# Four graph layers on one core: scores copied in halves of two batches, `gd` and `z` loads held to the product 40 back, the turned adjacency loaded beside layer one, partial rows added by VectorE

## The chip, the cores and the metric

The kernel runs on one core of one Trainium2 chip. The metric is the device time in microseconds; three runs give 3038.36, 3040.70 and 3043.71, a median of 3040.7 us. TensorE (PE) multiplies, VectorE (DVE) and ScalarE (ACT) work element by element, GpSimd (POOL) issues indirect DMAs (gathers and scatters by a list of rows) and SyncE (SP) issues most plain DMAs. All data are float32, and a product of the kernel appears in the trace as two matmuls.

## The reference, cut to what matters

`x` has 16 batches of 1024 nodes with 256 features; `adj` is 1024 x 1024 and sparse, with a diagonal. Four layers follow one another.

```python
# layer 0: a score for every edge
pre_u = h_t @ W1[:d]; pre_v = h_t @ W1[d:]
hidden = relu(pre_u[:, :, None, :] + pre_v[:, None, :, :] + b1)
S = sigmoid((hidden @ W2)[..., 0] + b2[0])
a_t = einsum('buv,bud->bvd', S * A_a, h_t)
m_t = einsum('uv,bud->bvd', A_m, h_t) * h_t
z = beta1 * h_t + beta2 * (a_t @ Wa + ba) + beta3 * (m_t @ Wm + bm)
# layer 1: neighbours
z = z + relu(einsum('ij,bjd->bid', adj, z) @ W.T + b)
# layers 2 and 3: attention with adj as the bias of the logits
feats = data @ W1.T; f1 = feats @ W2 + b2[0]
coefs = softmax(leaky_relu(f1[:, :, None] + f1[:, None, :]) + adj)
out = coefs @ feats + bias2 + data
```

## The kernel before, in words

The batches are taken in four groups of four (`GB = 4`). Layer 0's scores are worked out for edges alone: each node has 16 listed neighbours of its own (`FIRST`) and, where it has more, extra rows of four (`QUAD`). The score steps (`score_steps`) gather a neighbour's features (`z<-v_d`), take maxima and minima on VectorE (L1066 to L1068), add them up on ScalarE (L1034) and scatter the scores into one of two dense arrays in DRAM (`dense_d`, L951). They run as a side thread: `Side.along` lets the main work yield its estimated time and issues as many side steps as a pace allows. So the order of issue comes from the order of these generators, from explicit waits that hold an instruction to a product some places back (`paced(ins, back)`, 6 unless said otherwise), and from when buffers come free. Each engine, and each engine's own DMA queue, works in order.

A first stage (to about 906 us) does all that needs no score: it turns `adj` (`turn_adj`, into `adjT_d`, with its block sums in `sumT_d`), makes `m_t` and projects the features for all 16 batches (`hw_d`, `zb_d`). Its tiles (`own1`, `st`) are then given up, and their room goes to later pools. Then each group does, in order:

- **The scores** (`with_edges`, for group 3 `with_last_edges`). Four quarters `v` of 256 columns, in each eight steps `ut` of 128 rows. A step loads a block `gd` of scores from `dense_d` (`load_gd`, on SP, four buffers, held to the product 24 back), where the four batches lie interleaved; copies it into `gc`, batch by batch (ScalarE at L1499 for steps 0, 1, 3 and 5, VectorE at L1497 for 2, 4, 6 and 7, two buffers); and makes eight products with `hw`, two for each batch. After a quarter VectorE adds the eight sums to `z` (L1522). In some steps a load of `z` is issued behind the products, held to the product 12 back. Group 0 also loads the turned `adj` over `adj_sb` here (L1514, held to the product 16 back) and takes its exponential on ScalarE (L1484), for the attention layers.
- **Layer one**, for two batches at a time: `projected` makes y (8 steps), then seven block products (`neighbours_by_seven`, 28 steps) take the blocks of the turned `adj` from a stream of loads on SP (`adj_stream`): whole blocks into `blocks`, parts of 512 KB into `gc`, single pieces of 256 KB into `a`.
- **Two attention layers** (`fronts`, `sums`, `second`, `third`, in `group_layers`). A front's row of logits goes to DRAM and back, spread over all partitions (`to_row`, L1405 to L1407 on SP), and is used by `from_row` (L1412) some steps later. `later` holds calls that `tick` makes after a number of steps. The loads of the next group's `hw`, `z` and first four `gd` are issued here; `soon` asks for those `gd` between the halves of the group's last sums, if the next group's scores are all issued (`finished`).

The last group differs: two of its batches get layer one from lists (`by_lists`), beside the main work of the other two. 24 + 112 steps gather rows of y (`z<-y_d`) and add them, weighted, on VectorE (L1805, L1807); then 28 GpSimd DMAs (L1817) gather partial rows from `part_d` and add them into `msg` themselves (`compute_op=ALU.add`). Every step yields 1.0 and the main work gives 0.71 for each of its microseconds (`LISTED`). `from_lists` then turns `msg` on TensorE (L1830).

Of the kernel before, what the change touches and what calls it, by code (L numbers as in the profile page):

```python
# [81 lines left out]
def gnn_stack_kernel(  # L82
# [48 lines left out]
    recent = []  # L131
    BACK = 24

    def paced(ins, back=6):
# [6 lines left out]
    def product(*args, **kw):  # L141
        recent.append(nc.tensor.matmul(*args, **kw))  # L142
        del recent[:-BACK]
        return recent[-1]
# [780 lines left out]
    with tc.If(listed > 0) as arm:  # L925
        with ExitStack() as stack:
# [11 lines left out]
            gd_pool = stack.enter_context(tc.tile_pool(name="gd", bufs=4, reuse_waits="tile"))  # L938
            gc_pool = stack.enter_context(tc.tile_pool(name="gc", bufs=2, reuse_waits="tile"))
            searched = set()  # L940
# [230 lines left out]
            with ExitStack() as first:  # L1171
                own1 = first.enter_context(tc.tile_pool(name="own1", bufs=1, reuse_waits="tile"))
                st_pool = first.enter_context(tc.tile_pool(name="st", bufs=5, reuse_waits="tile"))
                side = Side(score_steps(own1))
                pools = (wide_t, wide_z)
# [10 lines left out]
                def spare_tile(tag):  # L1186
                    pool = dict(gd=gd_pool, gc=gc_pool)[tag]
                    shape = [P, QN, GB] if tag == "gd" else [P, GB, QN]
                    return pool.tile(shape, F32, tag=tag, name="sums").rearrange("p a b -> p (a b)")

                def last_plain(h, hT, mT):

                    for q, tag in ((S3, "gc"), (S1, "gd"), (S2, "gd")):
# [38 lines left out]
                def score_free():  # L1232
# [45 lines left out]
                    def first_turned(main):  # L1278
                        for us in itertools.islice(main, 4):
                            if turned_adj:  # L1280
                                what = turned_adj.pop(0)
                                if what[0] < HT - 1:
                                    room = [spare_tile("gc" if what[0] == 2 else "gd") for _ in range(2)]
                                else:
                                    room = list(ttile("sums")[:, : 2 * N].rearrange("p (k n) -> k p n", k=2))
# [59 lines left out]
                assert not zeros  # L1345

            two = stack.enter_context(tc.tile_pool(name="two", bufs=2, reuse_waits="tile"))
            three = stack.enter_context(tc.tile_pool(name="three", bufs=3, reuse_waits="tile"))
# [133 lines left out]

            def exponential(jt):
                paced(nc.scalar.activation(ea[:, jt, :], ea[:, jt, :], AF.Exp), 16)  # L1484

            def with_edges(g, hw, z):

                doing[0] = "edges"
                for v in range(N // QN):
                    cols = slice(v * QN, (v + 1) * QN)  # L1490
                    acc = [[bank() for _ in range(DH)] for _ in range(GB)]
                    for ut in range(NT):
                        gd = first_gd.pop(0) if first_gd else load_gd(g, v, ut, back=BACK)
                        gc = gc_pool.tile([P, GB, QN], F32, tag="gc", name="gc")
                        by_batch = gd.rearrange("p n i -> p i n")
                        if ut in (2, 4, 6, 7):
                            paced(nc.vector.tensor_copy(gc, by_batch), 16)  # L1497
                        else:
                            paced(nc.scalar.activation(gc, by_batch, AF.Copy), 16)  # L1499
                        for i in range(GB):  # L1500
                            for eh in range(DH):
                                product(
                                    acc[i][eh][:, :QN], hw[i][:, ut, eh * P : (eh + 1) * P], gc[:, i, :],
                                    start=ut == 0, stop=ut == NT - 1,
                                )
                        if z_loads and ut % 2 == 0:
                            load, *what = z_loads.pop(0)
                            paced(load(*what), 12)
                        if (to_load or to_exp) and ut % 2 and v:
                            if v > 1 and to_exp:  # L1510
                                exponential(to_exp.pop(0))
                            if to_load:
                                jt = to_load.pop(0)
                                paced(nc.sync.dma_start(ea[:, jt, :], adjT_d[jt]), 16)  # L1514
                                to_exp.append(jt)
                        yield 3.4 if g or v else 1
                    if v == N // QN - 1:
                        while to_exp:
                            exponential(to_exp.pop(0))
                    for i in range(GB):  # L1520
# [15 lines left out]
            def with_last_edges(g, hw, z, rows):  # L1536
# [27 lines left out]
                for v in (0, 2, 1, 3):  # L1564
# [8 lines left out]
                    for ut in range(NT):  # L1573
                        gd = first_gd.pop(0) if first_gd else load_gd(g, v, ut, back=BACK)
                        gc = gc_pool.tile([P, GB, QN], F32, tag="gc", name="gc")
                        by_batch = gd.rearrange("p n i -> p i n")
                        if v in held:
                            nc.vector.tensor_copy(gc[:, 2:, :], by_batch[:, 2:, :])
                            nc.scalar.activation(held[v][ut], by_batch[:, :2, :], AF.Copy)
                        elif ut in (2, 4, 6, 7):  # L1580
                            paced(nc.vector.tensor_copy(gc, by_batch), 16)
                        else:
                            paced(nc.scalar.activation(gc, by_batch, AF.Copy), 16)
                        for i in batches:
                            products(acc, i, ut, gc[:, i, :])
                        if z_loads and ut % 2 == 0:
                            load, *what = z_loads.pop(0)
                            paced(load(*what), 12)
                        yield 0.9 * len(batches)
# [72 lines left out]
            def adj_stream(room):  # L1662
# [14 lines left out]
                def ask(name, k, n=1, first=False):  # L1677
# [3 lines left out]
                    elif k < 2:  # L1681
                        a = gc_pool.tile([P, GB, QN], F32, tag="gc", name="adjT_in")
                        a, n = a.rearrange("p a b -> p (a b)").rearrange("p (k n) -> p k n", n=HN), 2
                    else:
# [85 lines left out]
            def by_lists(msg):  # L1770
# [13 lines left out]
                todo = [(NT + i, k) for i in range(XT) for k in range(QUAD)]  # L1784
                todo += [(t, k) for t in range(FAR) for k in range(FIRST)]
                got, stores, free = {}, [], []

                def fetch_row(t, k):
                    if not free:
                        free.extend(halves([slot_pool.tile([P, GB * R], F32, tag="z", name="z")]))  # L1790
                    z = got[t, k] = free.pop(0)
                    gather(z, y_d, lists(t)[1][:, k : k + 1])

# [5 lines left out]
                for n, (t, k) in enumerate(todo):  # L1799
# [3 lines left out]
                    to = msg[t] if t < NT else part[t % len(part)]  # L1803
                    if k == 0:
                        paced(nc.vector.tensor_scalar(to, z, lists(t)[3][:, k : k + 1], None, ALU.mult))  # L1805
# [8 lines left out]
                    yield 1.0  # L1814
                for q in range(NG):
                    for t in range(FAR):
                        gather(msg[t], part_d, to_u[:, q * NT + t : q * NT + t + 1], compute_op=ALU.add)  # L1817
                        yield 1.0

            def from_lists(z, msg):  # L1820
# [102 lines left out]
            def group_layers(g, z):  # L1923
# [21 lines left out]
                order = [(layer, i) for layer in range(2) for i in range(GB)]  # L1945
                yield from layer_one(z[:2])
                yield from fronts(0, 0, row=False)
                yield from layer_one(z[2:])
                for n, (layer, i) in enumerate(order):
                    if n + 1 < len(order):  # L1950
                        yield from fronts(*order[n + 1])
# [11 lines left out]
                catch_up()  # L1963

            def soon(g):

                if g in finished:
                    first_gd.extend(load_gd(g, 0, ut) for ut in range(4))

# [171 lines left out]
```

## Time and profile before

| what | value |
|---|---|
| median of three runs | 3040.7 us (3038.36 to 3043.71) |
| the profiled execution's own time | 3069.58 us |
| its span, first to last instruction | 3067.9 us |
| mean granted TensorE clock | 0.996 |
| TensorE matmul busy, weight load busy | 2990.1 us, 2140.8 us |
| VectorE, ScalarE, GpSimd busy | 2076.5, 1819.3, 1745.2 us |
| moved by DMA | 736.76 MB, 240 GB/s over the span |
| scores of groups 0, 1, 2, 3 | 909 to 1032, 1455 to 1574, 1998 to 2118, 2537 to 2641 us |
| end of the lists | 2849 to 2911 us |

How to read what is quoted. A row of waits gives the engine, the tile it wanted, who was waited for, then the time in all, how often, and the longest. A row of the timeline gives start, duration, engine (q: its queue, issuing a DMA), line, operation, tiles written and read, shapes, how many were merged, and in brackets the idle time ahead and who ended it. A row of windows gives the stretch, its length, busy time and count of PE, weight loads (PEld), VectorE, ScalarE and GpSimd, then the granted clock, the DMA share and GB/s. A row of groups gives line, engine, operation, tiles, shapes and count, then busy time and the mean of one in ns, then the idle time just before and what ended it. Most products have the line of a helper, L142.

### The profile page before, as it was taken

What the parts mean: (1) busy time and instruction counts of PE and PEld (TensorE: products, weight loads), DVE (VectorE), ACT (ScalarE), POOL (GpSimd) and SP (SyncE); (2) the same over time, 40 slices, a digit from 0 to 9 for tenths busy, and PEclk for the clock granted to TensorE, in tenths of its full rate; (3) what the DMA queues carried; (4) which work ended last, traced back from release to release, by engine and by line L of the source; (5) the groups of instructions that cost most, each with busy time, mean ns of one, the idle gap of its engine ahead of it and who ended that gap; (6) DMA issues with size and microseconds to landing.
All of it is one profiled execution on the core that took longest, in us unless ns stands there. A gap on an engine that the chain in (4) does not pass through costs nothing. (4 is left out here: it accounts for less than half of the span.)

```text
span 3067.9 us, 41621 instructions
## 1 busy us (share of the span) xinstructions
PE 2990.1 (97%) x11750; PEld 2140.8 (70%) x11750; DVE 2076.5 (68%) x4089; ACT 1819.3 (59%) x6466; POOL 1745.2 (57%) x1501
## 2 busy tenths in 40 slices
PE   8999999999999999999999999999999999999899
PEld 5545455555557657888775788787578888858787
DVE  8877566666665678887667788766777752478444
ACT  3437565667666767887766687776667733222342
POOL 1126577677654667667666767667666610467600
PEclk9999999999999999999999999999999999999999
DMA  9999999989899986578998666898866545676700
GB/s 296 315 353 329 306 306 301 278 251 279 252 337 342 298 265 183 173 215 283 301 294 270 188 181 194 284 306 288 273 195 167 151 159 181 230 234 175 144 1 29
DMA packets 324697, 736.76 MB, mean 240 GB/s; under 512 B 50973, under 2 KB 145242, under 8 KB 319338
## 3 DMA queue, kind: packets, MB, share of 16 engines
q0 software_dynamic: 131456, 394.14, 43.5%
q1 hardware_dynamic: 151610, 268.05, 26.3%
q10 hardware_dynamic: 41392, 71.84, 6.3%
q8 instruction: 94, 1.54, 0.2%
q14 instruction: 145, 1.19, 0.1%
HBM read 597.34 MB, written 136.53 MB: 239 GB/s over the span
## 5 line engine op out<-in xcount | busy, mean ns | idle before, releaser
L1034 ACT ACTIVATE z<-z 128x257 f32<-128x257 f32 x2432 | 984.1, 410 | 523.2 <-DVE z L1068 266.6
L142 PE MATMUL bank<-feats,m 128*128 128x257 f32 x4096 | 913.1, 381 | 13.9 <-DVE m L1465 4.5
L142 PEld LDWEIGHTS bank<-feats,m 128*128 128x128 f32 x4096 | 769.1, 190 | 128.6 <-DVE m L1465 6.7
L946 POOL DMA_INDIRECT z<-v_d,slot_v x512 | 606.4, 1184 | 403.4 <-ACT z L1034 162.4
L951 POOL DMA_INDIRECT dense_d<-gt,slot_at x512 | 588.1, 1149 | 221.7 <-PE bank L142 105.4
L1066 DVE TENSOR_TENSOR z<-z,u 128x580 f32<-128x580 f32 x608 | 460.9, 758 | 320.3 <-PE bank L142 228.5
L1465 DVE SCALAR_TENSOR_TENSOR m<-rho,tau,adj_sb 128x512 f32<-128x512 f32 x512 | 374.8, 745 | 143.2 <-PE bank L142 133.7
L1034 ACT ACTIVATION_READ_ACCUMULATOR z<-z 128x1 f32 x2432 | 467.2, 192 | 0.0
L142 PE MATMUL bank<-gc,hw 128*128 128x256 f32 x1920 | 422.2, 381 | 25.5 <-ACT gc L1499 20.3
L142 PEld LDWEIGHTS bank<-gc,hw 128*128 128x128 f32 x1920 | 361.3, 190 | 85.5 <-ACT gc L1499 28.0
L1067 DVE TENSOR_TENSOR z<-z,u 128x448 f32<-128x448 f32 x608 | 375.9, 618 | 0.0
L142 PE MATMUL bank<-w1p,hT 128*128 128x385 f32 x1024 | 340.1, 486 | 0.9 <-ACT hT L154 0.9
L142 PEld LDWEIGHTS bank<-w1p,hT 128*128 128x128 f32 x1024 | 193.1, 189 | 147.7 <-issue 22.0
L142 PE MATMUL bank<-g_wT,z 128*128 128x257 f32 x1024 | 231.3, 380 | 4.9 <-DVE z L1739 3.2
L142 PE MATMUL bank<-adj_sb,h 128*128 128x512 f32 x504 | 223.3, 593 | 0.1
L142 PEld LDWEIGHTS bank<-g_wT,z 128*128 128x128 f32 x1024 | 192.1, 190 | 36.5 <-issue 4.7
L373 ACT ACTIVATE st<-bank 128x385 f32<-128x385 f32 x256 | 122.3, 484 | 107.1 <-PE bank L142 67.7
L946 POOL DMA_INDIRECT z<-v_d,x_node x96 | 123.0, 1281 | 104.5 <-PE bank L142 43.9
L142 PEld LDWEIGHTS bank<-adj_sb,h 128*128 128x128 f32 x504 | 95.7, 190 | 115.6 <-issue 106.8
L1068 DVE TENSOR_TENSOR z<-z,sign 128x128 f32<-128x128 f32 x608 | 171.8, 283 | 0.0
L946 POOL DMA_INDIRECT z<-y_d,slot_v x112 | 124.0, 1107 | 45.8 <-issue 20.1
L142 PE MATMUL bank<-adjT_in,t 128*128 128x512 f32 x336 | 147.6, 592 | 0.0
(258 smaller groups left out, 3315.6 us busy)
## 6 DMA issues: line engine op xcount, KB each, us to landing
gd<-dense_d SPq DMA_DIRECT2D x128, 512.0 KB
dense_d<-zero ACTq DMA_DIRECT2D x64, 512.0 KB
h<-in_x_dram SPq DMA_DIRECT2D x19, 1024.0 KB
u_d<-st SPq DMA_DIRECT2D x128, 128.5 KB
v_d<-st SPq DMA_DIRECT2D x128, 128.5 KB
u<-u_d POOLq DMA_DIRECT2D x32, 514.0 KB
hw_d<-st SPq DMA_DIRECT2D x128, 128.0 KB
zb_d<-zb ACTq DMA_DIRECT2D x16, 1024.0 KB
```

The costliest lines, as they stand in the source:

```text
L142: recent.append(nc.tensor.matmul(*args, **kw))
L373: nc.scalar.activation(st[:, cols], ps[:, :half], AF.Copy)
L946: return paced(nc.gpsimd.indirect_dma_start(out=dst, out_offset=None, in_=src[:], in_offset=bass.IndirectOffsetOnAxis(ap=at, axis=0), **how,))
L951: return paced(nc.gpsimd.indirect_dma_start(out=dst[:], out_offset=bass.IndirectOffsetOnAxis(ap=at, axis=0), in_=src, in_offset=None,))
L1034: nc.scalar.activation(zk[:, c, :], zk[:, c, :], AF.Copy, accum_out=s[:, k, c : c + 1])
L1066: paced(nc.vector.tensor_tensor(big, big, uk[:, :, :BIG], ALU.max))
L1067: paced(nc.vector.tensor_tensor(low, low, uk[:, :, BIG:], ALU.min))
L1068: nc.vector.tensor_tensor(mixed, mixed, sign[:, None, :].to_broadcast([P, GB, MIXED]), ALU.mult)
L1465: nc.vector.scalar_tensor_tensor(m, r[:, cols], ta[:, kt : kt + 1], ea[:, kt, cols], ALU.max, ALU.mult)
```

## The change

- **Copies.** `gc` is now four buffers of two batches each, made after the first stage instead of before it, so that it lies where that stage's tiles were; the first stage's use of it goes to a pool `sums` of its own. Each step copies its scores in two halves on the same engine, held to the products 16 and 12 back, and a batch's products read the half that holds it. The stream's 512 KB loads into `gc` become two of 256 KB.
- **Holds.** The list of recent products keeps 40 (`DEEP`) instead of 24; `gd` and the `z` loads of the scores stages are held to the product 40 back, instead of 24 and 12.
- **Turned adj.** The eight loads and exponentials leave the scores of group 0 and go beside the first layer one of group 0 (`with_adj`): a load every fourth step, its exponential six steps later.
- **First gd.** `soon` is called from the sixth of a group's eight sums on, twice each, and issues the four loads once, spread over later steps.
- **Partial rows.** They are gathered into the tiles of the list steps, five steps ahead, and added into `msg` by VectorE.

The diff, its core:

```diff
+    DEEP = 40
     def product(*args, **kw):
         recent.append(nc.tensor.matmul(*args, **kw))
-        del recent[:-BACK]
+        del recent[:-DEEP]
...
-            gc_pool = stack.enter_context(tc.tile_pool(name="gc", bufs=2, reuse_waits="tile"))
...
+                sum_pool = first.enter_context(tc.tile_pool(name="sums", bufs=2, reuse_waits="tile"))
...
+            gc_pool = stack.enter_context(tc.tile_pool(name="gc", bufs=4, reuse_waits="tile"))
...
-            def exponential(jt):
-                paced(nc.scalar.activation(ea[:, jt, :], ea[:, jt, :], AF.Exp), 16)
+            def with_adj(main):
+                for n, us in enumerate(main):
+                    if n % 4 == 1 and to_load:
+                        jt = to_load.pop(0)
+                        paced(nc.sync.dma_start(ea[:, jt, :], adjT_d[jt]), 16)
+                        to_exp.append(jt)
+                    if n % 4 == 3 and len(to_exp) > (1 if to_load else 0):
+                        jt = to_exp.pop(0)
+                        paced(nc.scalar.activation(ea[:, jt, :], ea[:, jt, :], AF.Exp), 16)
+                    yield us
+
+            def by_batch(gd, ut):
+                gc = {}
+                for i in range(0, GB, 2):
+                    t = gc_pool.tile([P, 2, QN], F32, tag="gc", name="gc")
+                    scores = gd[:, :, i : i + 2].rearrange("p n i -> p i n")
+                    if ut in (2, 4, 6, 7):
+                        paced(nc.vector.tensor_copy(t, scores), 16 - 2 * i)
+                    else:
+                        paced(nc.scalar.activation(t, scores, AF.Copy), 16 - 2 * i)
+                    gc[i], gc[i + 1] = t[:, 0, :], t[:, 1, :]
+                return gc
...
                     for ut in range(NT):
-                        gd = first_gd.pop(0) if first_gd else load_gd(g, v, ut, back=BACK)
-                        gc = gc_pool.tile([P, GB, QN], F32, tag="gc", name="gc")
-                        by_batch = gd.rearrange("p n i -> p i n")
-                        if ut in (2, 4, 6, 7):
-                            paced(nc.vector.tensor_copy(gc, by_batch), 16)
-                        else:
-                            paced(nc.scalar.activation(gc, by_batch, AF.Copy), 16)
+                        gd = first_gd.pop(0) if first_gd else load_gd(g, v, ut, back=DEEP)
+                        gc = by_batch(gd, ut)
...
                         if z_loads and ut % 2 == 0:
                             load, *what = z_loads.pop(0)
-                            paced(load(*what), 12)
-                        if (to_load or to_exp) and ut % 2 and v:
-                            if v > 1 and to_exp:
-                                exponential(to_exp.pop(0))
-                            if to_load:
-                                jt = to_load.pop(0)
-                                paced(nc.sync.dma_start(ea[:, jt, :], adjT_d[jt]), 16)
-                                to_exp.append(jt)
+                            paced(load(*what), DEEP)
...
                     elif k < 2:
-                        a = gc_pool.tile([P, GB, QN], F32, tag="gc", name="adjT_in")
-                        a, n = a.rearrange("p a b -> p (a b)").rearrange("p (k n) -> p k n", n=HN), 2
+                        for i in range(2):
+                            a = gc_pool.tile([P, 2, QN], F32, tag="gc", name="adjT_in")
+                            a = ready[name, i] = a.rearrange("p a b -> p (a b)")
+                            load = nc.sync.dma_start(a, source(name)[:, i, :])
+                            if first:
+                                paced(load, BACK)
+                        return
...
                 todo += [(t, k) for t in range(FAR) for k in range(FIRST)]
+                todo += [(t, FIRST + q) for q in range(NG) for t in range(FAR)]
...
-                    gather(z, y_d, lists(t)[1][:, k : k + 1])
+                    if t < NT and k >= FIRST:
+                        at = (k - FIRST) * NT + t
+                        gather(z, part_d, to_u[:, at : at + 1])
+                    else:
+                        gather(z, y_d, lists(t)[1][:, k : k + 1])
...
-                    if k == 0:
+                    if t < NT and k >= FIRST:
+                        paced(nc.vector.tensor_tensor(to, to, z, ALU.add))
+                    elif k == 0:
...
-                for q in range(NG):
-                    for t in range(FAR):
-                        gather(msg[t], part_d, to_u[:, q * NT + t : q * NT + t + 1], compute_op=ALU.add)
-                        yield 1.0
...
-                yield from layer_one(z[:2])
+                yield from with_adj(layer_one(z[:2])) if g == 0 else layer_one(z[:2])
...
                 for n, (layer, i) in enumerate(order):
+                    if n >= 2 * GB - 3:
+                        soon(g + 1)
...
                     yield from sums(made[layer, i], 0, *ends)
-                    if n == 2 * GB - 1:
+                    if n >= 2 * GB - 3:
                         soon(g + 1)
...
             def soon(g):
-                if g in finished:
-                    first_gd.extend(load_gd(g, 0, ut) for ut in range(4))
+                if g in finished and g not in asked:
+                    asked.add(g)
+                    for ut in range(4):
+                        later.append([1 + 2 * ut, lambda ut=ut: first_gd.append(load_gd(g, 0, ut))])
```

More of the change, by code (lines that the diff above doesn't have):

```diff
@@ L1186, in spare_tile @@
                 def spare_tile(tag):
-                    pool = dict(gd=gd_pool, gc=gc_pool)[tag]
-                    shape = [P, QN, GB] if tag == "gd" else [P, GB, QN]
-                    return pool.tile(shape, F32, tag=tag, name="sums").rearrange("p a b -> p (a b)")
+                    pool = dict(gd=gd_pool, sums=sum_pool)[tag]
+                    return pool.tile([P, QN, GB], F32, tag=tag, name="sums").rearrange("p a b -> p (a b)")
                 def last_plain(h, hT, mT):
-                    for q, tag in ((S3, "gc"), (S1, "gd"), (S2, "gd")):
+                    for q, tag in ((S3, "sums"), (S1, "gd"), (S2, "gd")):
                         adj_sums[q] = [spare_tile(tag).rearrange("p (k n) -> p k n", n=HN) for _ in range(2)]
@@ L1282, in first_turned @@
                                 if what[0] < HT - 1:
-                                    room = [spare_tile("gc" if what[0] == 2 else "gd") for _ in range(2)]
+                                    room = [spare_tile("sums" if what[0] == 2 else "gd") for _ in range(2)]
                                 else:
@@ L1502, in with_edges @@
                                 product(
-                                    acc[i][eh][:, :QN], hw[i][:, ut, eh * P : (eh + 1) * P], gc[:, i, :],
+                                    acc[i][eh][:, :QN], hw[i][:, ut, eh * P : (eh + 1) * P], gc[i],
                                     start=ut == 0, stop=ut == NT - 1,
@@ L1507, in with_edges @@
                             load, *what = z_loads.pop(0)
-                            paced(load(*what), 12)
-                        if (to_load or to_exp) and ut % 2 and v:
-                            if v > 1 and to_exp:
-                                exponential(to_exp.pop(0))
-                            if to_load:
-                                jt = to_load.pop(0)
-                                paced(nc.sync.dma_start(ea[:, jt, :], adjT_d[jt]), 16)
-                                to_exp.append(jt)
+                            paced(load(*what), DEEP)
                         yield 3.4 if g or v else 1
-                    if v == N // QN - 1:
-                        while to_exp:
-                            exponential(to_exp.pop(0))
                     for i in range(GB):
@@ L1573, in with_last_edges @@
                     for ut in range(NT):
-                        gd = first_gd.pop(0) if first_gd else load_gd(g, v, ut, back=BACK)
-                        gc = gc_pool.tile([P, GB, QN], F32, tag="gc", name="gc")
-                        by_batch = gd.rearrange("p n i -> p i n")
+                        gd = first_gd.pop(0) if first_gd else load_gd(g, v, ut, back=DEEP)
                         if v in held:
[L1578 to L1581, printed above, removed]
+                            t = gc_pool.tile([P, 2, QN], F32, tag="gc", name="gc")
+                            nc.vector.tensor_copy(t, gd[:, :, 2:].rearrange("p n i -> p i n"))
+                            nc.scalar.activation(held[v][ut], gd[:, :, :2].rearrange("p n i -> p i n"), AF.Copy)
+                            gc = {2: t[:, 0, :], 3: t[:, 1, :]}
                         else:
-                            paced(nc.scalar.activation(gc, by_batch, AF.Copy), 16)
+                            gc = by_batch(gd, ut)
                         for i in batches:
-                            products(acc, i, ut, gc[:, i, :])
+                            products(acc, i, ut, gc[i])
                         if z_loads and ut % 2 == 0:
                             load, *what = z_loads.pop(0)
-                            paced(load(*what), 12)
+                            paced(load(*what), DEEP)
                         yield 0.9 * len(batches)
@@ L1945, in group_layers @@
                 order = [(layer, i) for layer in range(2) for i in range(GB)]
-                yield from layer_one(z[:2])
+                yield from with_adj(layer_one(z[:2])) if g == 0 else layer_one(z[:2])
+                assert not to_load and not to_exp
                 yield from fronts(0, 0, row=False)
@@ L1963, in group_layers @@
                 catch_up()
+            asked = set()
             def soon(g):
-                if g in finished:
-                    first_gd.extend(load_gd(g, 0, ut) for ut in range(4))
+                if g in finished and g not in asked:
+                    asked.add(g)
+                    for ut in range(4):
+                        later.append([1 + 2 * ut, lambda ut=ut: first_gd.append(load_gd(g, 0, ut))])
             def left_by(main):
```

## The prediction

> **What bounds the kernel now.** I read the page's busy table first, then TensorE's waits, then its timeline in the four scores stages and the tail, then the stage windows, and last the rows that price each edit.
>
> ```profile
> span 3067.9 us, 41621 instructions
> PE 2990.1 (97%) x11750; PEld 2140.8 (70%) x11750; DVE 2076.5 (68%) x4089; ACT 1819.3 (59%) x6466; POOL 1745.2 (57%) x1501
> ```
>
> TensorE (PE) is the bound: 2990.1 of 3067.9. No product is added or removed, so only the 77.8 us of idle time can shrink. Who ends it:
>
> ```profile
> PE bank L142 <- ACT gc L1499: 20.3, 16, 2.3
> PE bank L1830 <- DMA msg<-part_d,to_u: 9.8, 5, 3.6
> PE bank L142 <- DMA hw<-hw_d: 3.1, 1, 3.1
> ```
>
> The first two of these waits, the longest of all, are what the change touches: the ScalarE copy of the scores into `gc`, and the rows that a GpSimd DMA adds into `msg`. The stages, with PE busy ahead of the other engines:
>
> ```profile
> 909.00:1032.00 123.00, 110.45 (x503) 94.25 (x502) 69.40 (x129) 83.29 (x242) 60.01 (x50) 1.00 0.96 333
> 1032.00:1096.00 64.00, 64.00 (x187) 35.29 (x186) 43.93 (x85) 36.33 (x152) 43.20 (x39) 1.00 0.86 276
> 2537.00:2641.00 104.00, 104.00 (x486) 91.60 (x485) 30.39 (x53) 35.38 (x32) 1.01 (x2) 1.00 0.57 182
> 2849.00:2893.00 44.00, 43.67 (x218) 38.17 (x216) 20.44 (x42) 11.22 (x26) 36.13 (x23) 1.00 0.87 151
> 2892.60:2910.70 18.10, 8.14 (x34) 6.64 (x34) 5.46 (x10) 4.85 (x8) 8.36 (x6) 0.63 0.69 132
> ```
>
> They are the scores of group 0, its first layer one, the scores of group 3 (no score steps beside it, DMA 0.57, no idle at all), and the end of the lists. Summing the gaps in PE's timeline, the scores lose 12.55 us in group 0 (3.06 of it for `hw`), 6.32 in group 1 and 6.49 in group 2. In the waits above many carry ScalarE's name and are DMA waits underneath:
>
> ```profile
> 943.37 0.53 SPq L1163 DMA_DIRECT2D z<-zb_d  x1
> 945.10 0.33 SPq L1514 DMA_DIRECT2D adj_sb<-adjT_d  x1
> 945.52 5.38 SPq L1148 DMA_DIRECT2D gd<-dense_d  x2
> 947.78 2.02 ACT L1499 ACTIVATE gc<-gd 128x1024 f32<-128x1024 f32 x1 [2.09 <-DMA gd<-dense_d]
> 949.85 7.17 PE L142 MATMUL bank<-gc,hw 128*128 128x256 f32 x32 [1.75 <-ACT gc L1499]
> ```
>
> The SP queue holds a `z` load for the product 12 back and an `adj` load for the one 16 back, and the next `gd` waits behind them. Pairing issues with copies, a `gd` normally goes out 9.7 us before its first product and its copy starts 6.5 to 8.7 us after issue; between 938 and 972 in group 0 that takes 8.2 to 11.6 us, and one load early in each of groups 1 and 2 took 10.3 and 10.8. By cause the stalls are about 8.2 us of late `gd` (6.5 in group 0) and 14.1 us where the copy stood in ScalarE's queue.
>
> **The change part by part.** *gd and z at 40 back.* A product is two matmuls, 422.2/960 = 0.44 us, a step of eight products 3.5 us. 24 back gives 10 us of lead, 40 would give 17. Four `gd` buffers cap it at when the copy four steps earlier has ended, some 15 us. The worst landing above was 11.6, so the 8.2 us of late `gd` go. `z` at 40 back no longer holds what is behind it. Bounds: 0 (bandwidth alone sets the landing) to 8.2; I take 8, since 11.6 is well under 15.
>
> *Half copies.* Prices:
>
> ```profile
> L1499 ACT ACTIVATE gc<-gd 128x1024 f32<-128x1024 f32 x48 | 99.3, 2069 | 22.1 <-DMA gd<-dense_d 12.7 <-PE bank L142 6.8 <-issue 2.5
> L1579 ACT ACTIVATE held<-gd 128x512 f32<-128x512 f32 x16 | 18.2, 1138 | 28.1 <-DMA gd<-dense_d 27.9
> L1484 ACT ACTIVATE adj_sb<-adj_sb 128x1024 f32<-128x1024 f32 x8 | 8.4, 1046 | 0.0
> L1660 DVE TENSOR_TENSOR z<-z,r 128x512 f32<-128x512 f32 x8 | 5.5, 693 | 12.8 <-ACT r L1659 12.8
> ```
>
> Two halves cost ScalarE 2 x 1138 = 2276 ns for 2069, 0.2 us more on each of 56 copies, hidden where it is 68% busy. A whole copy could start only when the step two before had ended, leaving 3.5 - 2.07 = 1.4 us to spare. A half starts 1.7 us earlier and its user comes one half later: 3.5 + 1.7 - 1.14 = 4.1 us. No stall exceeded 2.3 us beyond the 1.4, 3.7 in all. But a copy also queues behind score sums, which are held to recent products, and at the ends of a quarter VectorE's eight adds to `z` come first: I take 8.5 of the 14.1 (bounds 0 and 14.1). The new buffers lie where `wm` lay and wait for its last products, some 1.2 us: hidden under the 3.06 us wait for `hw`, else that much.
>
> *Turned adj in layer one.* 8 loads of 0.52 MB and 8 Exp of 1.05 us leave the scores of group 0 (inside the above) and go beside 64 us with no PE gap. Each load waits for the product 16 back, 7 us old while y is projected and 14 in the seven products, so SP passes it at once. The loads ask for 4.19 MB/64 us = 66 GB/s beside 276 at share 0.86, so a share of about 1.07: some 4 us of transfers arrive later. Behind each on SP are the blocks of the adjacency stream, asked about two blocks (14 us) ahead. Bounds -1 to 12.6 us (4.19 MB at 333 GB/s, all exposed); I take +1. Splitting five 0.5 MB `gc` loads per layer one adds five issues of 0.3 to 0.4 us on SP, hidden there.
>
> *Early gd.* Scatters of group 1 end at 1355, of group 2 at 1921, so its first four loads move from one half ahead of the scores to three or four halves ahead, spread, past SP's `hw`, `z` and row loads. Idle at the two group ends is 9.0 us now; bounds -9 to +9; I take 0, the queue having 60 us for them. In group 3 the scatters end at 2470; a `gd` asked before that stands at SP's head until then, with `hw` and the row of the last front behind it, but that row goes out at 2484 now and `hw` has until 2537.
>
> *Partial rows by VectorE.* 28 GpSimd DMAs take 1.54 + 0.30 us each, 52 us from 2849 to 2902.5, and PE waits:
>
> ```profile
> 2892.07 0.60 PE L1880 MATMUL bank<-ident,z 128*128 128x128 f32 x4
> 2896.26 0.30 PE L1830 MATMUL bank<-ident,msg 128*128 128x128 f32 x1 [3.59 <-DMA msg<-part_d,to_u]
> ...
> 2910.64 8.99 PE L142 MATMUL bank<-g_wT,z 128*128 128x257 f32 x40
> ```
>
> From 2892.7 to 2910.6, 18 us pass for 32 transposes that take 0.13 us each elsewhere, 4.2 us. A plain gather of such a row takes 1.02 + 0.30 us (`z<-y_d`), under the 1/0.71 = 1.41 us of a list step, and is asked five steps ahead, so it keeps pace; the last add, 0.69 us, ends about 1 us after the stage's products. 18 - 4.2 - 1.8 = 12 us gained (9 if only the listed wait goes, 13.8 if all). The adds are 28 x 0.69 = 19.4 us on VectorE beside 20.44 of 44: 90%, more than the 80% of the list steps before (132.70 of 165). `m` for PE queues behind them: cost 1.5, bounds 0 and 5.
>
> In the last window the granted clock is 0.63, after a gap of 3.59 us; the gaps of up to 2.3 us in the scores left it at 1.00. [...]
>
> **The sum.** The profiled execution took 3069.58 (span plus 1.7): 8 + 8.5 + 12 - 1.5 - 1 = 26, so 3043.6 there. The median of the runs is 28.9 us shorter. If all of that is idle time, 49 of 77.8 us are left, so I count the scores' 16.5 at three quarters, 12.4; the tail follows from a fixed 1.84 us per DMA and counts whole. 12.4 + 12 - 2.5 = 21.9: 3040.7 - 21.9 = 3019.
>
> **Rivals.** *Bandwidth holds the scores* (0.22). For: shares of 1.02 to 1.03 in group 0 with landings up to 11.6 us, and 14 us of stalls in queues that an early copy does not shorten. Against: groups 1 and 2 run at 0.93, and most of their copies start 6.5 to 8 us after issue. Then the 40 does nothing that it says, and only the tail pays: 3040.7 - 12 + 2.5 = 3031. [...]
>
> *Nothing left* (0.10): as that, and `hw` and `z` loads queued later behind the early `gd` delay the row of the last front by about 3 us at each of three group ends: 3031 + 9 = 3040. Against: the 60 us above.
>
> *Slower: ScalarE parks on the moved Exp* (0.13). Each Exp comes six steps, 10.3 us, after its load. If landing takes longer, ScalarE, which works in order, stands there, and with it the evacuations of `y` and the first sums that PE's banks need. It decides from 10.3 us on; `hw` (1 MB) took up to 14.5 us at a share of 1.03. At 4 us for each of 8: 32 - 22 = 10 slower, 3051. Against: `gd`, of equal size, took longer than 10.3 us only three or four times in 96, and ScalarE has 28 of 64 us free there.
>
> **How the numbers follow.** Forecast 0.55, range of its own 3006 to 3029; 0.22 at 3031, 0.10 at 3040, 0.13 at 3051. The runs span 5.3 us, so 0.2%, 6 us, is about what can be told from no change: faster 0.55 + 0.22 = 0.77, same 0.10, slower 0.13. The range leaves out the slower case and a little at the bottom, where all idle of scores, tail and group ends goes: 3003 to 3044.
>
> **What would show it.** Right: PE's wait for ScalarE `gc` under 8 us, none over 1 us for `msg`, clock near 1.00 there, 28 new VectorE adds into `msg`, `gd` issued some 15 us ahead, layer one of group 0 still without gaps. Wrong: DMA `gd` still ending copies' waits; ACT idle until `adj_sb`; `m` waits in the last 40 us of the lists; row loads late at group ends.

## The result, and the profile after

The changed kernel takes 3017.02 us, the kernel before on the same chip 3039.53 us (medians): a ratio of 0.9931, 95% interval 0.9915 to 0.9947. At 3040 us that is 21 us less, with a bound of 16 to 26; 21.9 were forecast. The profiled execution took 3024.09 us, with a span of 3022.4. From the page:

```profile
PE 2980.0 (99%) x11750; PEld 2141.7 (71%) x11750; DVE 2106.4 (70%) x4173; ACT 1828.3 (60%) x6522; POOL 1724.1 (57%) x1501
```

TensorE's idle time fell from 77.8 to 42.4 us with the same 11750 matmuls. The two profiled spans differ by 45.5 us, over twice what the medians do, mostly because the profiled execution of before was 29 us longer than the median of its runs; so a difference between these two profiles is taken for a gain only where a run bears it out. TensorE's wait for the score copies, the row that answers to the first of before:

```profile
PE bank L143 <- ACT gc L1505: 2.7, 2, 1.4
```

The wait for ScalarE's `gc` went from 20.3 us to 2.7, the one for DMA `msg` from 9.8 to nothing, and that for `hw` from 3.1 to 0.5 (in the changed kernel's second profile it is 4.4, so it comes and goes). At the head of the list now stands a wait that was not there, 6.6 us once for VectorE's `z` of a layer one. The stages, with PE, weight loads, VectorE, ScalarE and GpSimd busy, granted clock, DMA share and GB/s:

```profile
906.80:1018.20 111.40, 110.88 (x513) 97.33 (x514) 70.94 (x144) 80.10 (x245) 60.47 (x50) 1.00 0.95 327
1018.20:1096.00 77.80, 71.24 (x207) 40.89 (x206) 48.28 (x93) 48.13 (x175) 52.40 (x41) 0.96 0.93 323
...
2813.60:2860.20 46.60, 45.71 (x226) 39.58 (x225) 36.59 (x66) 12.60 (x28) 29.81 (x27) 1.00 0.86 184
2860.20:2864.60 4.40, 3.87 (x34) 3.41 (x32) 3.28 (x8) 1.26 (x3) 0.00 (x0) 1.00 0.26 91
```

The scores of group 0 have half a microsecond of gaps left, at much the same DMA share as before (0.95, it was 0.96). The longer hold does what it was meant to: pairing each `gd` load with its first product (those behind the first four of a group, medians), the load goes out 15.7 us ahead of it where it went 9.9 ahead before, and the copies of ScalarE and VectorE wait 10.8 and 8.8 us in all for DMA `gd`, 12.7 and 44.5 before. Layer one of group 0 with the start of the front has lost time, at a clock of 0.96. VectorE is at 36.59 of 46.60 in the end of the lists, 79%, and the turn of `msg` takes 4.4 us at full clock. In the timeline its 32 transposes run from 2860.22 to 2864.47, with one gap of 0.40 us between.

The groups of instructions that pay for this, from the groups by line:

```profile
L1505 ACT ACTIVATE gc<-gd 128x512 f32<-128x512 f32 x112 | 126.4, 1138 | 65.0 <-PE bank L143 40.9 <-DMA gd<-dense_d 10.8 <-issue 6.4
...
L946 POOL DMA_INDIRECT z<-part_d,to_u x28 | 31.6, 1128 | 8.5 <-PE bank L143 4.9 <-issue 2.7 <-PE bank L1429 0.3
...
L1821 DVE TENSOR_TENSOR msg<-msg,z 128x512 f32<-128x512 f32 x28 | 19.2, 690 | 9.4 <-DMA z<-part_d,to_u 7.0 <-PE bank L143 1.6 <-PE bank L1843 0.9
```

A half copy takes the 1138 ns taken for it, an add 690, and one of the 28 gathers of partial rows 1128 ns where a gather that added mostly took 1540, 1575 on average.

### The profile page after: what moved, and what is told of

Same layout as the page of the kernel before. It is cut to its first block, busy times and chain, and to the rows that moved or that the text cites. A ratio compares the mean times of both kernels' runs of the same rounds, so it can differ in the third digit from the quotient of the medians.

```text
span 3022.4 us, 41916 instructions
## 1 busy us (share of the span) xinstructions
PE 2980.0 (99%) x11750; PEld 2141.7 (71%) x11750; DVE 2106.4 (70%) x4173; ACT 1828.3 (60%) x6522; POOL 1724.1 (57%) x1501
## 5 line engine op out<-in xcount | busy, mean ns | idle before, releaser
L951 POOL DMA_INDIRECT dense_d<-gt,slot_at x512 | 580.1, 1133 | 225.3 <-PE bank L143 126.1
L143 PE MATMUL bank<-w1p,hT 128*128 128x385 f32 x1024 | 340.4, 486 | 2.6 <-DVE sign L629 1.3
L1505 ACT ACTIVATE gc<-gd 128x512 f32<-128x512 f32 x112 | 126.4, 1138 | 65.0 <-PE bank L143 40.9
```

Source lines behind the costliest of these rows:

```text
L951: return paced(nc.gpsimd.indirect_dma_start(out=dst[:], out_offset=bass.IndirectOffsetOnAxis(ap=at, axis=0), in_=src, in_offset=None,))
L1505: paced(nc.scalar.activation(t, scores, AF.Copy), 16 - 2 * i)
```

## The experiments

They were run in three sets, each on a chip of its own, on which the kernel before took 3036, 3058 and 3069 us. So ratios to before on the same chip are compared, and turned into microseconds of 3040. A difference of two ratios is uncertain by about 0.002, 6 us, in the first two sets, and by about 0.003, 9 us, in the third. The ranges of the expectations are on the scale of the first result, 3017.0 us, so a time is put beside them as 3017 plus its distance from the changed kernel.

### The partial rows alone undone

```diff
-                todo += [(t, FIRST + q) for q in range(NG) for t in range(FAR)]
+                for q in range(NG):
+                    for t in range(FAR):
+                        gather(msg[t], part_d, to_u[:, q * NT + t : q * NT + t + 1], compute_op=ALU.add)
+                        yield 1.0
```

> The changed kernel, but the 28 partial rows are again added by GpSimd's gathers into msg; all else as changed (3017.0 us). Theory (GpSimd's 28 gathers with an add, 1.84 us each in the kernel before, end after the lists and the msg transposes wait for them): the PE waits for DMA msg come back (9.8 us in the profile before), VectorE loses 28 adds of 0.69 us, and the time rises by 9.5 us (12 less the 2.5 us charged for the adds) to 3026.5, between 3023 and 3030. Rival (the msg turn got shorter because the lists stage ahead of it ended differently, with earlier copies and freer queues): the msg turn stays under 7 us and the time is within 3 us of 3017.

Measured: 3028.08 us, ratio 0.9977 (0.9965 to 0.9988), 0.0046 above the changed kernel, 14 us. TensorE's waits and the window of the turn:

```profile
PE bank L1847 <- DMA msg<-part_d,to_u: 9.6, 5, 3.2
```

```profile
2853.70:2866.80 13.10, 6.72 (x33) 5.14 (x34) 3.17 (x5) 3.87 (x6) 5.67 (x4) 0.63 0.77 139
```

The wait is back almost to the tenth of before (9.8), and so is the clock of 0.63. The edit is worth 14 us, a little above the theory's range; the rival falls. By the profiles of this set, the last sums and the turn of `msg` together took 61.8 us here and 50.2 to 50.5 in the other three, 11 to 12 us.

### Turned adj back in the scores, and its loads alone

```diff
-                yield from with_adj(layer_one(z[:2])) if g == 0 else layer_one(z[:2])
+                yield from layer_one(z[:2])
```

with the lines of before in `with_edges` again.

> The changed kernel, but the 8 loads of turned adj and their 8 Exp are back in the scores of group 0, every second step. Theory (the move is about a wash: the scores of group 0 gained 14.0 us in the profile where those of group 1 gained 7.7, so about 6 us are the move's; layer one of group 0 lost 9.5 us to late gathers of z): the scores of group 0 get 4 to 8 us longer, the stretch from layer one to the front 6 to 9 us shorter, and the time is 3014 to 3019. Rival one (with gd held 40 back the loads would hurt nothing in the scores any more): scores of group 0 within 2 us, time 3008 to 3012, so the move itself was a loss. Rival two (the loads and Exp are what made the scores of group 0 late, and the layer-one loss is chance): 3021 to 3026.

Measured: 3010.87 us, ratio 0.9924 (0.9910 to 0.9938), 2 us below the changed kernel, which is less than the uncertainty. The scores of group 0 took 112.1 us against 111.4, the stretch behind layer one 7.0 against 16.4. In the scores rival one is right: with `gd` held 40 back the loads cost nothing there. The next run puts only the loads back and leaves the Exp in layer one.

> The changed kernel, but the 8 loads of turned adj are back in the scores of group 0, every second step; the 8 Exp stay in layer one of group 0. Theory (the loads, 0.5 MB each, are what makes the gathers of z late there, VectorE waits for these in order, and TensorE for VectorE): layer one of group 0 up to the front 7 to 8 us, the time as with both back, 3010 to 3014. Rival (the Exp hold up ScalarE, and so the normalisation that VectorE waits for): layer one still 12 to 16 us, the time 3015 to 3018.

Measured: 3034.76 us, ratio 0.9918 (0.9905 to 0.9930), 4 us below, and the stretch took 7.0 us. So by the profiles the loads cost something beside layer one and the Exp alone do not; both times are within the uncertainty of the changed kernel's. The changed kernel's timeline shows how:

```profile
1039.55 1.06 ACT L1493 ACTIVATE adj_sb<-adj_sb 128x1024 f32<-128x1024 f32 x1 [3.21 <-DMA adj_sb<-adjT_d]
...
1070.63 4.93 POOL L946 DMA_INDIRECT z<-v_d,slot_v  x1 [0.30 <-DMA z<-v_d,slot_v]
...
1082.24 0.77 DVE L1066 TENSOR_TENSOR z<-z,u 128x580 f32<-128x580 f32 x1 [4.40 <-DMA z<-v_d,slot_v]
...
1090.23 3.34 PE L143 MATMUL bank<-g_wT,z 128*128 128x257 f32 x7 [6.56 <-DVE z L1750]
```

A gather of the score steps is late (GpSimd takes 4.93 us over one, where most take about 1), VectorE stands on it in order for 4.40 us and at the next two for 1.51 and 1.37, and behind it in its queue is the last sum of layer one, which TensorE's front needs. ScalarE does park on a moved Exp, 3.21 us in the first row, but TensorE has no gap from 1018 us to the front. With whole copies (below) ScalarE stood on three of these loads for 8.5 us together, and the stretch still took 7.0. The size varies: this stretch took 7.0 us in all five profiles with the loads in the scores (both of before among them), and 16.4, 8.1, 9.4, 13.4, 9.3, 7.0, 15.5, 12.3 and 8.6 in the nine with the loads in layer one, 11.1 on average. The move costs some 4 us by the profiles; the times alone do not show it.

### The holds undone, and the hold of z alone

```diff
-    DEEP = 40
+    DEEP = 24
...
-                            paced(load(*what), DEEP)
+                            paced(load(*what), 12)
```

> The changed kernel, but gd is held to the product 24 back and z to 12 back as in the kernel before; half copies and their buffers stay. Theory (half of the gain in the scores, 12.4 us in the timed runs, is the lead of gd): landing again 9.7 us after issue instead of the 15 us ahead of need, copies start late, the waits for ScalarE's and VectorE's gc copies come back in part: 3021 to 3026, likeliest 3023. Rival one (the halves alone give the slack: a product then needs only its half copy): 3016 to 3019. Rival two (the hold is what matters, the halves only spread the same copy): 3026 to 3031.

Measured: 3022.57 us, ratio 0.9949 (0.9935 to 0.9963), 5.5 us above, in the theory's range but no more than the uncertainty. The profile, of the slowest of its five executions (3031.19 us), shows the mechanism: a `gd` goes out 9.7 us before its first product again, the copies of ScalarE and VectorE wait 55.0 and 32.5 us for DMA `gd`, and TensorE 11.6 us for ScalarE's `gc`. In group 0:

```profile
948.64 0.53 SPq L1163 DMA_DIRECT2D z<-zb_d  x1
...
950.40 6.96 SPq L1148 DMA_DIRECT2D gd<-dense_d  x2
...
955.15 1.11 ACT L1505 ACTIVATE gc<-gd 128x512 f32<-128x512 f32 x1 [7.54 <-DMA gd<-dense_d]
...
956.31 2.00 PE L143 MATMUL bank<-gc,hw 128*128 128x256 f32 x8 [2.95 <-ACT gc L1505]
```

The `z` load goes out first, the `gd` behind it, ScalarE stands 7.54 us on DMA `gd`, TensorE 2.95 on ScalarE: the picture of before.

> The changed kernel, but z is again held to the product 12 back, gd stays at 40. Both holds undone gave 0.9949 of before against 0.9931. Theory (gd's lead carries it, z only fills group ends): 0.992 to 0.994, waits for ScalarE's gc under 4 us in all. Rival (z at 12 stands in SyncE's queue ahead of the next gd and so delays gd itself): 0.994 to 0.996, waits for gc of 6 us or more.

Measured: 3048.40 us, ratio 0.9936 (0.9914 to 0.9957), waits for `gc` of 1.6 us, and 3.3 and 8.7 us of copies waiting for DMA `gd`. With `gd` at 40 back, the hold of `z` changes nothing that can be told: `gd`'s lead is enough. Whether `z` at 40 back would be enough without it was not run.

### Whole copies again

```diff
-            gc_pool = stack.enter_context(tc.tile_pool(name="gc", bufs=4, reuse_waits="tile"))
+            gc_pool = stack.enter_context(tc.tile_pool(name="gc", bufs=2, reuse_waits="tile"))
...
-                for i in range(0, GB, 2):
-                    t = gc_pool.tile([P, 2, QN], F32, tag="gc", name="gc")
+                t = gc_pool.tile([P, GB, QN], F32, tag="gc", name="gc")
```

> The changed kernel, but scores are copied whole again into two buffers of four batches, and the later layers load turned adj into them 512 KB at a time; gd and z stay held to the product 40 back. Theory (the other half of the gain in the scores is the finer copy): waits for ScalarE's gc of 5 to 9 us are back in the scores, 3020 to 3026, likeliest 3023. Rival one (with the lead of 40 products the whole copy is done in time as well: ScalarE was not late of itself): 3016 to 3019. Rival two (two buffers are the bound whatever the lead): 3027 to 3031. The two undone edits should add to 12.4 us if neither covers the other; if each alone is under 4 us, they cover each other.

Measured: 3028.94 us, ratio 0.9983 (0.9973 to 0.9992), 16 us above, 3033 on the scale of the expectation: above the theory's range and even rival two's. But two buffers are not the bound everywhere, and here no copy of ScalarE or VectorE into `gc` waits for DMA `gd`. The scores of groups 0 and 1 stayed short (112.4 and 114.5 us), those of group 2 took 129.2. There:

```profile
1983.35 0.76 DVE L1066 TENSOR_TENSOR z<-z,u 128x580 f32<-128x580 f32 x1 [4.35 <-DMA z<-v_d,slot_v]
...
1984.88 0.42 ACT L1034 ACTIVATE z<-z 128x257 f32<-128x257 f32 x1 [4.95 <-DVE z L1068]
...
1990.52 2.01 ACT L1503 ACTIVATE gc<-gd 128x1024 f32<-128x1024 f32 x1
...
1992.58 1.22 PE L143 MATMUL bank<-gc,hw 128*128 128x256 f32 x2 [8.34 <-ACT gc L1503]
```

VectorE waits 4.35 us for a late gather, ScalarE 4.95 for VectorE, the whole copy stands behind those sums in ScalarE's queue, and TensorE stands 8.34 us. With halves the same queue exists; the changed kernel's longest gap in these scores was 1.50. The late gather itself seems to go with another edit, the early `gd` of the next section. It was issued at 1973.73, 9.6 us before VectorE used it; with the late `gd` and half copies the same gather went out 14.0 us ahead and VectorE did not wait for it. So part of the 16 us may be the early `gd`'s: whole copies with the late `gd` were not run.

> The changed kernel with both edits of the scores undone: gd held 24 back, z 12 back, whole copies into two buffers. The one alone cost 5.6 us, the other alone 11.9. Theory (each gives its own slack, and the two add): 3033 to 3037. Rival one (the prediction's sum, 12.4 us for both together, the edits cover each other): 3028 to 3031. Rival two (they need each other, so the loss is larger than the sum): over 3038.

Measured: 3054.60 us, ratio 0.9990 (0.9975 to 1.0004), 18 us above the changed kernel; TensorE's waits:

```profile
PE bank L143 <- ACT gc L1503: 17.1, 11, 3.6
```

The two alone made 5.5 + 15.8 = 21 us, both together 18: within the uncertainty they add, as the theory said (3035 on its scale), though 12.4 is not excluded. In the profile nearly all of before is back: the scores of groups 0 to 2 took 361.8 us in all, 363.9 in before, 340.4 in the changed kernel.

### The first gd late again

```diff
-                    if n >= 2 * GB - 3:
-                        soon(g + 1)
...
-                    if n >= 2 * GB - 3:
+                    if n == 2 * GB - 1:
                         soon(g + 1)
...
-                    for ut in range(4):
-                        later.append([1 + 2 * ut, lambda ut=ut: first_gd.append(load_gd(g, 0, ut))])
+                    first_gd.extend(load_gd(g, 0, ut) for ut in range(4))
```

> The changed kernel, but the first four gd of a group are again issued at once at the start of its scores, and the gathers' descriptors again at the group's last step. Theory (with two buffers of two batches more and holds of 40 there are later copies enough; what is first in the scores is set by hw): 3015 to 3019. Rival one (the early issue is what removed the waits in the first 15 us of the scores of groups 0 and 1): 0.5 to 3 us of waits each at the start of the three scores, 3020 to 3026. Rival two (the early gd takes bandwidth from the sums of the group before): 3010 to 3014.

Measured: 3024.67 us, ratio 0.9897 (0.9881 to 0.9913), 0.0034 below the changed kernel, 10 us; on the same chip the changed kernel took 3037.81. On the scale of the expectation that is 3007: the theory falls, and the early issue is a loss, in the direction of rival two and larger than its range. GpSimd's timeline at the end of group 1, the changed kernel, then this one:

```profile
1921.50 1.55 POOL L951 DMA_INDIRECT dense_d<-gt,slot_at  x1 [3.93 <-DVE m L1466]
...
1935.40 1.25 POOL L951 DMA_INDIRECT dense_d<-gt,slot_at  x1 [10.85 <-PE bank L143]
```

```profile
1912.43 1.52 POOL L951 DMA_INDIRECT dense_d<-gt,slot_at  x1 [0.30 <-issue]
...
1919.91 1.09 POOL L951 DMA_INDIRECT dense_d<-gt,slot_at  x1 [4.69 <-PE bank L143]
```

The first row is the first scatter of group 3, the other its second. `Scatters.add` keeps a dependency on the first scatter, so the second waits until it has landed; the product that the bracket names had ended long before. From the end of the first one's issue to the start of the second, 12.4 us pass with the early `gd` and 6.0 with the late ones. Four `gd` of 512 KB and three `hw` of 1 MB fill the DMA engines in just that stretch:

```profile
1920.00:1940.00 20.00, 17.86 (x87) 15.02 (x86) 15.84 (x39) 13.47 (x50) 6.51 (x5) 1.00 1.04 378
```

```profile
1905.00:1925.00 20.00, 20.00 (x97) 17.38 (x96) 15.02 (x34) 18.11 (x70) 9.89 (x10) 1.00 0.83 278
```

The DMA share is 1.04 in the changed kernel and 0.83 with the late `gd`. GpSimd gets 5 instructions done in 20 us instead of 10, and in the changed kernel's second profile its next 14 scatters were 9 to 12 us further behind TensorE's products than in this one, before it caught up. Gathers that come late are what VectorE, and with it ScalarE and TensorE, then stand on, as in the run with whole copies (4.35, 4.95 and 8.34 us). Place and spacing are told apart by a run with the late place and the spaced issue:

> The changed kernel, but the first four gd of a group wait for the middle of the group's last step again; there they still go out one by one. Theory (what costs is their place: at the earlier place four gd of 512 KB and three hw of 1 MB fill the queues just when the first scatter of group 3 has to land, and GpSimd parks 10.9 to 14.3 us on it in all eight profiles with the early place, 4.6 us in the two with the late one): GpSimd waits under 6 us for that scatter, the time is 0.989 to 0.991 of before as with u_soon. Rival (what helped was that all four go out at once): GpSimd waits 4 to 6 us as well, but the time stays at 0.992 to 0.994.

Measured: 3041.92 us, ratio 0.9917 (0.9894 to 0.9941): inconclusive in time. All profiles together, with the kernels whose copies and `gd` hold are as changed (end of group 1: the last sums before the scores of group 2):

| first four gd | GpSimd's wait for the first scatter, us | end of group 1 + scores of group 2, us |
|---|---|---|
| early, spaced (six profiles) | 10.9, 14.0, 14.2, 14.3, 11.2, 11.0 | 182.1, 184.9, 183.6, 181.7, 185.5, 188.0 |
| late, at once (two) | 4.7, 4.1 | 176.1, 175.6 |
| late, spaced (one) | 5.2 | 181.7 |

The wait goes with the place, as expected. The time of the two stages does not follow it as clearly: 181.7 us with the late place and the spacing is as short as the shortest of the early ones, and on its own chip it lies between 188.0 (early) and 175.6 (late, at once). So the parked GpSimd is shown, and the loss is shown; that the one is the whole cause of the other is not. How the 10 us divide between place and spacing stays open.

### The changed kernel and the one before once more

> The changed kernel itself once more, beside the others on the same chip. Expected 3014 to 3019 (0.993 of the kernel before). In its profile two stretches are to be looked at again: layer one of group 0 up to the front (16.4 us in the first profile, 9.4 with the partial rows undone, 7.0 with adj back in the scores) and the scores of group 2 (117.5 us). Theory: the loss in layer one comes from gathers that the loads of adj delay by a varying amount, so it varies from run to run between 2 and 10 us. Rival: it is 16.4 us again and fixed.

Measured: 3037.81 us, ratio 0.9931 (0.9917 to 0.9946), the same ratio on another chip. The stretch behind layer one took 8.1 us, the scores of group 2 114.9: both vary, as the theory said.

> The kernel before once more, for a second profile: its first profiled execution took 3069.6 us where its other runs took 3040.7. Theory (part of the waits in the first profile are of that execution alone): the execution is within 0.4% of the other runs of before, the wait for DMA msg is 8 to 11 us and that for ScalarE's gc over 10 us again, but the front behind the last layer one takes about 15 us and not 22.8. Rival (those waits are of the kernel): the front takes 20 us or more again.

Measured: one execution of 3076.46 us, where the other runs of before on that chip had a median of 3069.11. Its waits:

```profile
PE bank L142 <- ACT gc L1499: 19.3, 13, 2.5
PE bank L1830 <- DMA msg<-part_d,to_u: 9.5, 6, 3.3
```

The two waits that the change removes are there again, almost to the microsecond. The front behind the last layer one took 23.5 us, so the theory falls in this point and the rival holds: that stage was slow in both profiles of before. The last section compares it with the changed kernel's on the same chip.

### Both losses undone

> The changed kernel with two of its edits undone together: adj's loads and Exp back in the scores of group 0, and the first four gd of a group issued at once at the group's last step. Half copies, holds of 40 and VectorE's adds stay. Theory (the two losses are in different stages, 0.0007 and 0.0034 of the time of before, and add to the 0.9931 of the changed kernel): 0.988 to 0.991 of before, faster than every kernel so far. Rival (the early gd and the early adj loads compete for the same DMA time, so only one of them is won back): 0.990 to 0.993.

Measured: 3034.36 us, ratio 0.9886 (0.9862 to 0.9910), against 0.9931 for the changed kernel: another 14 us, the lowest ratio of all, and below the changed kernel's interval. The scores of group 0 took 110.6 us with no gap over 0.25, although adj is loaded there again. The three edits that are left (half copies, the hold of 40, VectorE's adds) make the whole gain. Against the late `gd` alone (0.9897) the difference is 0.0011, less than the uncertainty, so the times do not show that the second loss adds to the first.

## Why the prediction was right, and where it was not

The time came out within 2 us, and that closeness is luck: two gains were sized too small, by 5.6 and 3.5 us, and a loss of 10 us was put at nothing. The mechanism of the two gains was right.

- **Late gd and copies**, 8 and 8.5, counted at three quarters, 12.4. The mechanism is right: the waits for `gc` fell to 2.7 us, under the 8 named, and `gd` goes out 15.7 us ahead, as the "some 15" said. The size was low, with 18 us for both undone (bound about 11 to 25). By the times the halves carry more of it than the hold, 16 against 5.5, where the prediction had them about equal; but the scores of groups 0 to 2 took 356.1 us in the profile with whole copies, the fastest of its executions, and 355.0 in that with the holds undone, the slowest, so the share of each is not settled. Scaling by three quarters had no ground: the second profile of before, on another chip, belongs to an execution 7 us longer than the first and has 21 us of gaps in the scores instead of 25. How long an execution of before is does not tell how large those gaps are. The wait for `wm`'s last products, charged at nothing, does not show: the scores of group 0 have one gap, 0.52 us.
- **Tail**, 12 less 1.5 for the adds. Measured 14. The turn of `msg` takes 4.4 us, near the 4.2 worked out, at a clock of 1.00 instead of 0.63. The price of the adds didn't come: the sums beside them took 46.6 us, 49.0 before, and all waits for `m` in the profile are 2.1 us, with VectorE busy for 79% where 90% was reckoned.
- **Turned adj**, +1 with bounds up to 12.6. Measured +2 and +4, both within the uncertainty, some +4 by the profiles. The transfers were the cost, as the prediction took it (its share of 1.07 came out as 0.93); who pays was not named: the score steps' gathers, then VectorE in order, then TensorE's front.
- **Early gd**, 0 with bounds of -9 to +9. This is the step that failed: it costs 10 us (bound about 4 to 17). What was reckoned with, "the queue having 60 us for them", was the room in SyncE's queue and TensorE's idle time at the group ends, and not who else needs the DMA engines there: GpSimd stood 10.9 to 14.3 us on one scatter instead of 4.1 to 5.2.
- **The rivals.** Bandwidth holding the scores falls: the DMA share of group 0's scores is 0.95, it was 0.96 before, and the gaps are gone. That the 40 does nothing, as this rival had it, does not hold: the copies' waits for DMA `gd` fell from 57.2 to 19.6 us. At the end of group 1 GpSimd's scatter pays for SyncE's loads: GpSimd waits 10.9 us for it where the early loads take the DMA share to 1.04, and 4.7 us at 0.83 with the late ones. ScalarE parking on the moved Exp did happen, 3.21 us on DMA `adj_sb`, one of the signs that the prediction had named as wrong; it cost TensorE no gap in layer one, and with whole copies 8.5 us of it left the stretch at 7.0. So it is not what made the loss there.

By the runs, the sum is 18 + 14 - 2 to 4 - 10 = 18 to 20 us, and 21 (16 to 26) were measured for the whole. The prediction had 12.4 + 12 - 2.5 for the same terms.

## What to carry to other kernels

The early issue of `gd` cost 10 us here although its own queue had room: look at the DMA share of the stretch that an issue is moved into (here 1.04, against 0.83 with the late loads), and at the small transfer there that someone waits for in order (here one scatter, 10.9 us against 4.7, and one gather, 4.35 us). When copies stand in the queue of an engine that also serves other work, halving them with the same bytes of buffer lets the next engine start on the first half (1.14 us, where a whole copy took 2.07); here that was worth up to 16 us, and issuing the loads earlier some 5, neither of them settled to better than 6 us. A change of five edits should be taken apart even if its time is as forecast: by the last run two of the five here lost 14 us of the 35 that the others won.

## What was not expected of the hardware

**The clock after a gap.** The prediction read a granted clock of 0.63 after the gap of 3.59 us in the tail, and of 1.00 after those of up to 2.3 us in the scores. The profiles show no line between the two by length: in the 3.5 us after a gap the granted clock was 0.64 after 2.6 us (holds undone) and 0.50 after 3.22 (partial rows undone), but 1.00 after gaps of 2.95 (holds undone), 3.06 (before, at 912) and 3.7 (the changed kernel's second profile). The profile of before has both after gaps of one length, 2.47 us, which end at 1409.79 and at 2753.21 (each row is the 3.3 us behind one):

```profile
1409.80:1413.10 3.30, 3.30 (x14) 2.63 (x15) 2.57 (x8) 2.46 (x11) 1.09 (x2) 1.00 0.81 244
```

```profile
2753.20:2756.50 3.30, 3.29 (x9) 2.26 (x10) 3.30 (x6) 3.30 (x10) 0.74 (x1) 0.61 0.42 127
```

After each of the ten gaps of 4.17 to 8.34 us behind the start, in all 14 profiles together, it was 0.50 to 0.63. So the 0.63 in the tail cannot be put down to the length of its gap alone; that the turn of `msg` ran at 1.00 without that gap is measured. What decides after gaps of 2.47 to 3.7 us was not shown.

**One stage that goes with the chip.** The front behind the last layer one takes 14.9 us in all four profiles of the first set, 18.1 to 20.8 in the second and 18.9 to 23.5 in the third, with little regard to the kernel: on the third chip 18.9 to 22.9 with the change and 23.5 before. So the 7.7 us by which the first two profiles differ there (22.8 and 15.1) cannot be put down to the change; the chip of the first profile of before is not on record. Why the stage differs is open.
